# Two-layer masked attention network on one core: where W1's loads and sums are issued in the first steps, and one scaling of Wq folded into a sum

## The chip, the cores and the metric

The kernel runs on one core of one Trainium2 chip. The metric is the device time of one execution in microseconds (us), lower is better. The kernel before was timed three times; the profiled execution is a fourth run with a time of its own.

## What is computed

`x` holds 128 graphs of 128 nodes with 512 features, `adj` one 128x128 mask for each graph. Two layers follow each other:

```python
q = (x @ Wq + bq);  k = (x @ Wk + bk);  v = (x @ Wv + bv)      # 8 heads of 64
logits = einsum('bqhd,bkhd->bhqk', q, k) / sqrt(64)
attn = softmax(where(adj > 0, logits, -1e9), axis=-1)
out = relu(einsum('bhqk,bkhd->bqhd', attn, v) @ Wo + bo)
x = layernorm(x + out)                                         # layer 0

Wh = x @ W1;  s_i = Wh @ a[:512];  s_j = Wh @ a[512:]
e = where(adj > 0, leaky(s_i[:, :, None] + s_j[:, None, :]), -9e15)
x = layernorm(x + leaky(softmax(e, axis=1) @ Wh))              # layer 1
```

Everything is float32.

## The kernel before

**Products.** Every 512x512 weight is cut into four blocks of 256x256, and a product with it is done in seven block products instead of eight, by a Strassen scheme. For this the weight needs three further blocks and one changed one, made once: `right_blocks` (L149 to L156) takes places 0 to 3 (the loaded blocks) and computes `t2 -= t0`, `t5 = t3 - t2`, `t4 = t5 - t0`, `t6 = t1 - t5`, one VectorE instruction each (L152 to L155). `PLACE` says which place each of the seven products reads. The activations need four such sums too (`left_blocks`, L275 to L278), and these are on GpSimd. A chain of seven products writes three PSUM banks, called y, w and x; between products a bank is copied out by ScalarE (`read`, L343 or L347, and L458) or added to such a copy by VectorE (`add`, L384), and TensorE may go on with that bank only after this. For brevity p1, p5, p6, p2, p7, p4, p3 are the products of a chain in their order of issue, and c11, c22, c21, c12 the four results. c22 reads bank w before p3 goes on adding to it.

**Steps.** The main loop (`for t in range(-3, END)`) has one step per graph. Groups of four graphs share the products for Q, K and V (`group_product`, L366, 8 records each of these products in the trace); pairs of graphs share those with Wo and W1 (`pair_product`, L447). A step t issues the scores of graph t (L518), its mask sums, maxima, exponentials (L552), reciprocals (L562) and divisions (L566), stores the softmax weights to DRAM (`sm.store`, L573), fetches them back in another order (`sm.fetch`, L579: `paz`), and in step t + 1 transposes them on VectorE (L583: `paT`) and multiplies them with V (L596). `group()`, `pair()` calls between these pop pieces of the product chains.

**Order.** The order on every engine is the order in which the program issues (`manual_schedule`), so each engine's queue is in order and a waiting instruction holds what stands behind it. All loads and stores but the first four go through SyncE's queue, in program order. One-time work that isn't urgent lies in a list `chores`; `group()` pops two of them at a time in steps t >= 0 (three at t = -3).

**Around the change.**
- W1: `load_w1` (L190) returns ten loads (two broadcasts of the halves of `a`, L196, then eight quarter-column loads of W1, L124) and a list of sums: eight `dots` (L205, two VectorE instructions each with an accumulator read behind each: products of W1's rows with `a`), four `last_column` (L220, two small adds each) and the four block sums. Here W1 is stored with 257 columns per half, the last one holding these dot products, so its block sums are 128x514. The loads go to `chores` at t = 0. The sums are popped by `w1_chores`: four `dots` after the maxima of step 3 and four at its middle, the `last_column` at the middle of step 5, the block sums late in step 5.
- Wv's seven blocks live in DRAM and come back through a ring of three buffers (`wv_n`, L407), fetched ahead of each product.
- Wq: at the start `scale` (L944) multiplies each loaded block by 1/8 on VectorE. `other_half` runs behind the first issued product: it transposes graphs 2 and 3, then scales place 2, makes `t2 -= t0`, issues the four GpSimd sums of x (`add_x`), scales place 3 and makes the other three block sums. In the first group Q's products are issued in the order p1, p2, p5, p6, p7.

Of the kernel before, what the change touches and what calls it, by code (L numbers as in the profile page):

```python
# [24 lines left out]
def kernel(  # L25
# [120 lines left out]

    PLACE = (0, 1, 3, 6, 2, 5, 4)

    def right_blocks(t):  # L149

        return [
            lambda: nc.vector.tensor_sub(t[2], t[2], t[0]),  # L152
            lambda: nc.vector.tensor_sub(t[5], t[3], t[2]),
            lambda: nc.vector.tensor_sub(t[4], t[5], t[0]),
            lambda: nc.vector.tensor_sub(t[6], t[1], t[5]),  # L155
        ]  # L156

    def places(w):
# [31 lines left out]
    def load_w1():  # L190

        a_b = [work.tile([P, D], F32, name="a_b", tag="wh", bufs=4) for _ in range(2)]

        def load_a(s):
            half = a1[s * D : (s + 1) * D].rearrange("f o -> (f o)")
            return lambda: nc.sync.dma_start(a_b[s], half.partition_broadcast(P))  # L196

        loads = [load_a(0), load_a(1)] + block_loads(W1, columns(w1), nc.sync)
        sums = small.tile([P, 2, 2, 2, 2], F32, name="wa", bufs=1)

        def dots(k, o, c):
            def run():
                for s in range(2):
                    scr = work.tile([P, HALF], F32, name="wa_scr", tag="x1S")
                    nc.vector.scalar_tensor_tensor(  # L205
                        scr,
                        w1[:, 2 * o + k, c, :HALF],
                        1.0,
                        a_b[s][:, o * HALF : (o + 1) * HALF],
                        op0=ALU.mult,  # L210
                        op1=ALU.mult,
                        accum_out=sums[:, s, k, o, c : c + 1],
                    )

            return run

        def last_column(k, o):
            def run():
                for c in range(2):
                    nc.vector.tensor_add(  # L220
                        w1[:, 2 * o + k, c, HALF:],
                        sums[:, o, k, 0, c : c + 1],
                        sums[:, o, k, 1, c : c + 1],
                    )

            return run

        every = [(k, o) for k in range(2) for o in range(2)]
        ops = [dots(k, o, c) for k, o in every for c in range(2)]
        return loads, ops + [last_column(k, o) for k, o in every] + right_blocks(places(w1))  # L230

    X, XT, XS, Q, K, V, MF, OT, X1T, X1, WH = ({} for _ in range(11))

# [709 lines left out]
    def scale(n):  # L943
        nc.vector.tensor_scalar_mul(wq[:, n], wq[:, n], QSCALE)  # L944

    wq_sums = right_blocks(places(wq))
    turned = [order_features(b) for b in range(2)]
    keep_busy(14)
# [10 lines left out]
    def other_half():  # L959

        for b in (2, 3):
            transpose_rows(b, order_features(b), nc.scalar.copy)
        scale(2)
        wq_sums[0]()
        add_x()
        scale(3)
        for op in wq_sums[1:]:
            op()

    chores += right_blocks(places(wk)) + load_wv()  # L970
    END = B - GROUP
# [2 lines left out]
    for t in range(-3, END):  # L974
        pair_steps = []
        if t % GROUP == 1 and on(t + 3):
            rest = group_steps
            group_steps, v_pieces, fetch_v = products((t + 3) // GROUP)
            group_steps = rest + group_steps
        if t % 2 == 1 and on(t - 3):  # L980
            pair_steps = zero[(t - 3) // 2] = LayerZero((t - 3) // 2)
            pair_steps = pair_steps.steps()
        if t % 2 == 0 and on(t - 6):
            pair_steps = LayerOne((t - 6) // 2).steps()

        def group(n=1):
            for _ in range(min(n, len(group_steps))):
                group_steps.pop(0)()
            for _ in range(min((3 if t == -3 else 2 if t >= 0 else 1) * n, len(chores))):
                chores.pop(0)()  # L990

        def w1_chores(n):
            for op in [w1_sums.pop(0) for _ in range(n)]:
                op()

        def pair(n=1):
            for _ in range(min(n, len(pair_steps))):
                pair_steps.pop(0)()

        if on(t + 1):  # L1000
            load_mask(t + 1)
        if t == 0:
            load_blocks(Wo, columns(wo), nc.sync, spread_rows=False)
            late_chores = right_blocks(places(wo)) + load_bias()
            w1_loads, w1_sums = load_w1()
            chores += w1_loads
        if t == 1:
            chores += late_chores

        last, sm = sm, Softmax(t, first_homes if t in (0, 2, 4) else None) if on(t) else none  # L1010
        sm.scores()
        coming.turn_blocks()
        if t % 2 == 1 and on(t - 3):
            zero[(t - 3) // 2].by()
            zero[(t - 3) // 2].bw()
        if later and t > 4:
            later.pop().go_back()
        if t == 5:
            group(2)
        if t < 3:  # L1020
            sm.maxima()
            group(2)
            if on(t - 2):
                load_residual(t - 2)
            if t == 0 and on(GROUP):
                sum_x(1)()
            sm.exp(0, 1, 2, 3)
            group()
            sm.reciprocals(0)
            sm.exp(4, 5, 6, 7)  # L1030
            if t == 1:
                group()
            sm.reciprocals(1)
            sm.divide(0, 1, 2, 3)
            last.transpose()
            group()
            sm.divide(4, 5, 6, 7)
            if t == 1:
                group()
            if on(t + 1):  # L1040
                mask_float(t + 1)
        elif t == 4:

            layer = later.pop()
            sm.maxima()
            group()
            layer.apply(0)
            load_residual(2)
            if on(8):
                sum_x(2)()  # L1050
            sm.exp(0, 1)
            group()
            sm.exp(2, 3, 4, 5)
            last.transpose()
            group()
            layer.store(1)
            layer.store(0)
            layer.fetch(1)
            layer.fetch(0)
            sm.exp(6, 7)  # L1060
            group()
            sm.reciprocals(0)
            sm.reciprocals(1)
            sm.divide(0, 1, 2, 3, 4, 5, 6, 7)
            mask_float(5)
        else:
            sm.maxima()
            group()
            if t == 3:
                w1_chores(4)  # L1070
            if t == 5:
                turn_x1(4)
                x1_sums()
            edge = coming
            edge.add()
            fin.residual()
            if on(t - 2):
                load_residual(t - 2)
            edge.maxima()
            fin.stats()  # L1080
            fin.rstd()
            x1_sums()
            if t % GROUP == 0 and on(t + GROUP):
                sum_x(t // GROUP + 1)()
            pair()
            sm.exp(0, 1, 2, 3)
            edge.exp()
            if t in (3, 5):
                w1_chores(4)
            pair()  # L1090
            sm.exp(4, 5)
            last.transpose()
            group()
            sm.reciprocals(0)
            pair()
            sm.exp(6)
            fin.apply()
            fin.store()
            sm.exp(7)
            edge.divide()  # L1100
            pair()
            sm.reciprocals(1)
            sm.divide(0, 1, 2, 3)
            coming = Edge(t - 6) if on(t - 6) and t + 1 < END else none
            coming.sender()
            coming.store_sender()
            if t == 5:
                w1_chores(4)
            group()
            sm.divide(4, 5)  # L1110
            pair()
            sm.divide(6, 7)
            if on(t + 1):
                mask_float(t + 1)
            group()
        sm.store()
        if t >= 6:
            coming.fetch_sender()
        sm.fetch()
        for b in x_turns(t):  # L1120
            transpose_x(b)
        for b in x_turns(t + 1):
            load_x(b)
        if on(t + 1):
            mask(t + 1)
        pair(2)
        if t % 2 == 0 and on(t - 6):
            turn_x1(t)
        if t not in (0, 4):
            group(21 if t % GROUP == 0 else 1)  # L1130
        fin = edge
        fin.product()
        fin.copy()

        last.attend()
        last.copy()
        if t % 2 == 0:
            last.sum(0, 1, 2, 3)
# [183 lines left out]
```

## Time and profile before

| | |
|---|---|
| three timed runs | 2402.37 us median (2400.96 to 2404.64) |
| profiled execution | 2402.25 us, of which 2400.4 us are the profile's span |
| TensorE matmul / weight load busy | 98% / 82% of the span |
| VectorE, ScalarE, GpSimd busy | 76%, 63%, 34% |
| data moved | 395.32 MB, 165 GB/s on average |

The page gives busy times of the engines, a chain of what ended last, groups of instructions and DMA issues. The waits view names, for an engine, what it waited for, with the total, the count and the longest. The timeline lists instructions in order: start in us, duration in us, engine, line, operation, tile written <- tiles read, shape, count, and in brackets the idle time before it with its releaser. The windows view gives busy time of each engine in a stretch, then the granted TensorE clock as a share of full speed, the DMA engines' busy share and GB/s. In the trace tile names have lost their digits, so W1 is `w`, and the layer-0 buffers X1 are `x`. Scores of step 0 begin at 41.0 us, of step 1 at 49.2, step 2 at 69.3, step 3 at 80.6, step 4 at 102.3, step 5 at 111.6 and step 6 at 132.9.

### The profile page before, as it was taken

Reading aid. Unit: us, or ns where it says so; the run is one execution under the profiler, and the core shown is the slowest. Engines: PE = TensorE matmul, PEld = TensorE weight load, DVE = VectorE, ACT = ScalarE, POOL = GpSimd, SP = SyncE. Lnnn points to the kernel's source line nnn. Section 1 sums busy time; section 2 is a strip of 40 time slices with the busy share of each in tenths; the row PEclk is TensorE's granted clock in tenths of the full one; section 3 lists DMA queues with packets and bytes.
Section 4 is the critical chain, followed back from the end, with each engine's and each line's share of the span. In section 5 each row is a group of like instructions: output and inputs, shape, how many; then the busy total and the mean of one; then the engine's idle time right before and its main releaser. Section 6 shows DMA issues by size and latency. Waiting matters only on the chain.

```text
span 2400.4 us, 44153 instructions
## 1 busy us (share of the span) xinstructions
PE 2363.4 (98%) x13362; PEld 1980.3 (82%) x13362; DVE 1827.0 (76%) x3719; ACT 1517.3 (63%) x5463; POOL 811.1 (34%) x1195
## 2 busy tenths in 40 slices
PE   8999999999999999999999999999999999999996
PEld 7888888888888888888888888888888888888874
DVE  5677787777777877877777778778778777777777
ACT  3666666566666666665666666666666666666685
POOL 1232333233333333332333433333323334333335
PEclk9999999999999999999999999999999999999999
DMA  7455555555546545555545555555554554554452
GB/s 205 158 165 160 174 163 162 176 161 158 179 147 186 164 154 174 160 165 181 159 154 183 154 176 167 156 173 157 169 181 157 157 179 155 173 175 151 156 170 98
DMA packets 435566, 395.32 MB, mean 165 GB/s; under 512 B 108280, under 2 KB 339328, under 8 KB 435328
## 3 DMA queue, kind: packets, MB, share of 16 engines
q1 hardware_dynamic: 435008, 392.23, 52.3%
q8 instruction: 107, 1.75, 0.3%
q14 instruction: 131, 1.07, 0.1%
q10 hardware_dynamic: 320, 0.26, 0.0%
HBM read 248.58 MB, written 143.72 MB: 163 GB/s over the span
## 4 chain that ended last, share of the span: by engine, by line
PE 91%; DVE 3%; DMA 2%; ACT 2%; issue 1%; SPq 1%; POOL 1%; DVEq 0%; ACTq 0%; POOLq 0%
PE st_y L366 27%; PE p_y L447 17%; PE st_w L366 13%; PE p_w L447 9%; PE st_x L366 7%; PE lg L518 6%; PE p_oT L596 5%; PE p_x L447 4%; PE p_h L837 4%; DMA wv_n<-wv 1%; ACT pa L552 0%; DMA x_dram<-x 0%; DMA wq<-in_L_gnn_Wq_dram 0%; ACT pa L566 0%; POOL rstd L648 0%
## 5 line engine op out<-in xcount | busy, mean ns | idle before, releaser
L552 ACT ACTIVATE pa<-pa,nmax 128x128 f32<-128x128 f32 x1008 | 392.6, 393 | 5.9 <-DVE nmax L541 5.5
L646 POOL TENSOR_SCALAR ve<-mv 128x1 f32<-128x1 f32 x256 | 69.9, 273 | 855.9 <-DVE mv L642 847.1
L566 ACT ACTIVATE pa<-pa,rs 128x128 f32<-128x128 f32 x1008 | 334.1, 395 | 8.6 <-DVE rs L562 8.5
L275 POOL TENSOR_TENSOR oS<-oT 128x256 f32<-128x256 f32 x63 | 45.8, 727 | 643.4 <-ACT oT L610 643.4
L532 DVE TENSOR_TENSOR pa<-lg,mf 128x512 f32<-128x512 f32 x252 | 161.9, 684 | 99.9 <-PE lg L518 99.6
L458 ACT COPY pr_t<-p_y 128x257 f32<-128x257 f32 (+1 forms) x375 | 137.7, 367 | 135.7 <-PE p_y L447 133.3
L343 ACT COPY st_t<-st_y 128x512 f32<-128x512 f32 x192 | 110.5, 575 | 144.2 <-PE st_y L366 143.1
L552 ACT ACTIVATION_READ_ACCUMULATOR pa<-pa,nmax 128x1 f32 x1008 | 192.3, 191 | 0.0
L347 ACT ACTIVATE st_t<-st_y,b_cols 128x256 f32<-128x256 f32 x192 | 80.6, 471 | 164.9 <-PE st_y L366 164.9
L648 POOL TENSOR_TENSOR rstd<-ve,mhalf 128x1 f32<-128x1 f32 x256 | 177.0, 691 | 21.4
L596 PEld LDWEIGHTS p_oT<-paT,v 128*64 128x64 f32 x2016 | 107.5, 136 | 91.8 <-PE st_y L366 44.0
L610 ACT ACTIVATE oT<-p_oT,b_cols 128x128 f32<-128x128 f32 x504 | 144.2, 368 | 60.0 <-PE p_oT L596 58.9
L583 DVE STREAM_TRANSPOSE paT<-paz 128x1024 f32<-128x1024 f32 x126 | 156.9, 1245 | 3.3 <-DMA paz<-pa_dram 2.1
L541 DVE TENSOR_REDUCE nmax<-pa 128x8 f32<-128x1024 f32 x126 | 153.7, 1220 | 4.4
L518 PE MATMUL lg<-kT,qT 64*128 64x128 f32 x2048 | 148.7, 285 | 0.0
L518 PEld LDWEIGHTS lg<-kT,qT 64*128 64x128 f32 x2048 | 124.2, 187 | 22.9 <-issue 22.9
L596 PE MATMUL p_oT<-paT,v 128*64 128x128 f32 x2016 | 137.9, 279 | 0.3 <-DVE paT L583 0.3
L768 DVE TENSOR_TENSOR wh<-p_w,pr_t 128x257 f32<-128x257 f32 x122 | 51.9, 425 | 104.0 <-PE p_w L447 64.1
L447 PE MATMUL p_y<-wo,oT 128*128 128x256 f32 x504 | 129.9, 380 | 0.7 <-ACT pr_t L458 0.6
L447 PE MATMUL p_y<-wo,oS 128*128 128x256 f32 x504 | 129.4, 379 | 0.0
L447 PE MATMUL p_y<-w,x1T 128*128 128x257 f32 x496 | 128.2, 381 | 0.2 <-DVE x1T L245 0.2
L447 PE MATMUL p_y<-w,x1S 128*128 128x257 f32 x496 | 128.0, 380 | 0.0
(201 smaller groups left out, 6032.8 us busy)
## 6 DMA issues: line engine op xcount, KB each, us to landing
pa_dram<-pa SPq DMA_DIRECT2D x126, 512.0 KB, 3.0
paz<-pa_dram SPq DMA_DIRECT2D x504, 128.0 KB, 2.8
wv_n<-wv SPq DMA_DIRECT2D x224, 256.0 KB, 2.8
x<-in_x_dram SPq DMA_DIRECT2D x128, 256.0 KB, 2.9
x_dram<-x SPq DMA_DIRECT2D x128, 256.0 KB, 2.5
xz<-x_dram SPq DMA_DIRECT2D x512, 64.0 KB, 2.0
xz<-in_x_dram SPq DMA_DIRECT2D x496, 64.0 KB, 2.2
out_dram<-z SPq DMA_DIRECT2D x120, 256.0 KB, 2.3
```

The lines of the kernel that those rows point to most:

```text
L366: nc.tensor.matmul(p[:, m, :], lhs, rhs, start=start and m == 0 and kc == 0, stop=True, skip_group_check=True,)
L447: nc.tensor.matmul(p[:, :width], xs()[n][:, kc, :], w[:, PLACE[n], kc, :], start=start and kc == 0, stop=True, skip_group_check=True,)
L458: nc.scalar.copy(t[:, :width], p[:, :width])
L518: nc.tensor.matmul(self.lg[r][:, c, :], q[rows, c, cols], k[rows, c, cols], start=c == 0, stop=True, skip_group_check=True,)
L532: nc.vector.tensor_add(by_head[:, r * NC : (r + 1) * NC], self.lg[r].rearrange("p c (b k) -> p c b k", b=4), mf.unsqueeze(1).to_broadcast( ...
L541: nc.vector.tensor_reduce(self.nmax, by_head, AX.XY, ALU.max, negate=True)
L552: nc.scalar.activation(self.pa[:, :, h, :], self.pa[:, :, h, :], AF.Exp, bias=self.nmax[:, h : h + 1], accum_out=self.sums[:, h : h + 1],)
L566: nc.scalar.activation(self.pa[:, :, h, :], self.pa[:, :, h, :], AF.Copy, scale=self.rs[:, h : h + 1])
L583: nc.vector.transpose(self.paT.rearrange("p h (a i) -> p a h i", i=32), self.paz.rearrange("p a (h k) -> p a h k", k=32),)
L596: nc.tensor.matmul(self.oT[r * HD : (r + 1) * HD, c, :], v[:, h * HD : (h + 1) * HD], self.paT[:, r * NC + c, :], start=c == 0, stop=True, ...
L610: nc.scalar.activation(OT[pair][:, c, h * P : (h + 1) * P], self.oT[:, c, :], AF.Identity, bias=b_cols[:, 1, c : c + 1],)
L648: nc.gpsimd.tensor_tensor(self.r, ve, mhalf, ALU.pow)
```

## The change

Four edits, all in what is issued before step 6:
1. W1's loads leave `chores`. Four are issued behind the store of the softmax weights of step 0, four behind that of step 1, the last two behind that of step 2; in each step ahead of the fetch.
2. W1's `dots` are done in three places: three after the maxima of step 3, two late in step 3 (behind the divisions of heads 0 to 3), three at the end of the first half of step 4. Since each pops two instructions, these are 6, 4 and 6 VectorE instructions. The four `last_column` move to late in step 5.
3. W1's four block sums are issued on GpSimd, right behind the `last_column`.
4. For Wq, the scalings of places 2 and 3 are folded into the sums that follow them: t2 and t5 each become one instruction that multiplies by 1/8 and subtracts. Place 3 is still scaled, now after all sums. The GpSimd sums of x are issued behind the first of the two.

```diff
-    def right_blocks(t):
+    def right_blocks(t, engine=nc.vector):
 
         return [
-            lambda: nc.vector.tensor_sub(t[2], t[2], t[0]),
-            lambda: nc.vector.tensor_sub(t[5], t[3], t[2]),
-            lambda: nc.vector.tensor_sub(t[4], t[5], t[0]),
-            lambda: nc.vector.tensor_sub(t[6], t[1], t[5]),
+            lambda: engine.tensor_sub(t[2], t[2], t[0]),
+            lambda: engine.tensor_sub(t[5], t[3], t[2]),
+            lambda: engine.tensor_sub(t[4], t[5], t[0]),
+            lambda: engine.tensor_sub(t[6], t[1], t[5]),
         ]
...
-        return loads, ops + [last_column(k, o) for k, o in every] + right_blocks(places(w1))
+        ops += [last_column(k, o) for k, o in every]
+        return loads, ops, right_blocks(places(w1), nc.gpsimd)
...
+    def scaled_less(n, left, right):
+
+        nc.vector.scalar_tensor_tensor(
+            wq[:, n], wq[:, left], QSCALE, wq[:, right], op0=ALU.mult, op1=ALU.subtract
+        )
+
...
             transpose_rows(b, order_features(b), nc.scalar.copy)
-        scale(2)
-        wq_sums[0]()
+        scaled_less(2, 2, 0)
         add_x()
+        scaled_less(5, 3, 2)
+        for op in wq_sums[2:]:
+            op()
         scale(3)
-        for op in wq_sums[1:]:
-            op()
...
-            w1_loads, w1_sums = load_w1()
-            chores += w1_loads
+            w1_loads, w1_sums, w1_blocks = load_w1()
...
             layer.fetch(0)
+            w1_chores(3)
             sm.exp(6, 7)
...
             if t == 3:
-                w1_chores(4)
+                w1_chores(3)
...
             edge.exp()
-            if t in (3, 5):
-                w1_chores(4)
             pair()
...
             coming.store_sender()
+            if t in (3, 5):
+                w1_chores(2 if t == 3 else 4)
             if t == 5:
-                w1_chores(4)
+                for op in w1_blocks:
+                    op()
             group()
...
         sm.store()
+        if 0 <= t < 3:
+            for load in w1_loads[4 * t : 4 * t + 4]:
+                load()
         if t >= 6:
             coming.fetch_sender()
         sm.fetch()
```

## The prediction

> **What bounds the kernel now.** I read first the windows of the whole run, since the change touches only the first 135 us and I must know whether a gain there survives.
>
> ```profile
> 60.00:180.00 120.00, 115.61 (x670) 97.81 (x670) 84.02 (x185) 75.46 (x282) 31.94 (x42) 0.98 0.51 162
> 180.00:2280.00 2100.00, 2099.46 (x11937) 1767.30 (x11936) 1620.24 (x3287) 1343.15 (x4868) 713.18 (x1029) 1.00 0.53 166
> 2280.00:2400.40 120.40, 97.94 (x517) 73.10 (x515) 92.40 (x202) 80.26 (x262) 54.59 (x110) 0.95 0.40 133
> ```
>
> The second column is the length, the third TensorE's busy time. From 180 to 2280 us TensorE is idle for 0.54 us in all: a TensorE-bound stretch, in which an earlier start is kept. Only its idle time and its slow clock before that can be won. Second, TensorE's waits in the first 200 us:
>
> ```profile
> PE st_w L366 <- DVE kT L384: 2.8, 1, 2.8
> PE st_w L366 <- DMA wv_n<-wv: 2.8, 1, 2.8
> PE st_w L366 <- DMA wk<-in_L_gnn_Wk_dram: 2.6, 1, 2.6
> ```
>
> Three waits of 2.6 to 2.8 us; all others are below 1.4. Third, the timeline around each, VectorE and GpSimd at the start, then SyncE and TensorE at 46, then VectorE and TensorE at 92:
>
> ```profile
> 12.03 1.33 DVE L944 TENSOR_SCALAR wq<-wq 128x512 f32<-128x512 f32 x1 [2.26 <-DMA wq<-in_L_gnn_Wq_dram]
> 13.39 1.63 DVE L152 TENSOR_TENSOR wq<-wq 128x512 f32<-128x512 f32 x1
> ...
> 18.13 0.69 DVE L154 TENSOR_TENSOR wq<-wq 128x512 f32<-128x512 f32 x1
> ```
>
> ```profile
> 46.24 0.91 SPq L196 DMA_DIRECT2D a_b<-in_L_gnn_a_dram  x2
> 47.20 0.90 SPq L124 DMA_DIRECT2D w<-in_L_gnn_W_dram  x2
> 48.20 0.37 SPq L407 DMA_DIRECT2D wv_n<-wv  x1
> ```
>
> ```profile
> 56.05 2.67 PE L366 MATMUL st_w<-wv_n,xT 128*128 128x256 f32 x8 [2.78 <-DMA wv_n<-wv]
> 58.51 2.92 PE L366 MATMUL st_y<-xT,wq 128*128 128x256 f32 x8
> ```
>
> ```profile
> 92.04 0.42 DVE L205 SCALAR_TENSOR_TENSOR wa_scr<-w,a_b 128x256 f32<-128x256 f32 x1
> 92.39 0.08 DVE L205 DVE_READ_ACCUMULATOR wa_scr<-w,a_b 128x1 f32 x1
> 92.39 1.24 DVE L583 STREAM_TRANSPOSE paT<-paz 128x1024 f32<-128x1024 f32 x1
> 93.55 0.65 DVE L384 TENSOR_TENSOR kT<-st_w,st_t 128x512 f32<-128x512 f32 x1
> ```
>
> The first wait is put down to a DMA, but st_w at 15.12 reads place 2 of Wq, ready at 13.39 + 1.63 = 15.02: it is VectorE's chain. The second is the last Wv block, issued behind four W1 loads and landing after 7.7 us where the median of its kind is 2.8. The third is K's c22, behind sixteen dot products on VectorE. After each of the three the windows show a granted clock of 0.5 for about 3 us, and none after the waits of 0.9 and 1.0 us at 51 and 21 us.
>
> **What the Trainium skill says.**
> - "TensorE: Matmul & The Clock Gate", Part 1: the array's clock halves after an idle window of about 3.4 us, which runs freely, and comes back after about as much work. The trace agrees on half and on the recovery (0.50 between 57 and 60 us), but waits of 2.6 to 2.8 us are already enough here.
> - "DMA: Bandwidth & Descriptors", Queues, rings and completion order: descriptors on one DMA engine are taken in ring order, so on SyncE's queue an earlier load goes first. The 7.7 us agree.
> - "SBUF — State Buffer", Who interferes with whom: a VectorE instruction with two SBUF inputs and a GpSimd instruction that reads SBUF exclude each other; the second one waits. The trace agrees: the 128x512 subtraction took 1.63 us beside GpSimd's sums of x, 0.69 after them.
> - "GPSIMD Engine Reference", section 3: a tensor_tensor is about 2 times slower there. In the trace GpSimd's 128x512 sums take 1.27 us alone, against 0.69.
>
> **The change, part by part.** Times are those of the profiled execution (2402.25 us).
>
> *Wq.* Until 17.5 us GpSimd is busy with four sums (ends 13.07, 14.47, 16.15, 17.55), and VectorE's four instructions end 0.3 to 0.55 us behind these ends: it advances one instruction for each GpSimd sum, whatever its kind. So I take the folded instructions at the same pace, and not at their bare 0.69: t2 ends at 13.6 instead of 15.02, t5 at 15.0 instead of 18.09, t4 at 16.7, t6 at 18.1, the scaling 0.38 later. p5 starts at 13.7 (TensorE free since 12.49, a wait of 1.2 us, too short to halve the clock), p6 at 15.45, p7 after ScalarE's copy (0.98 us as before) at 18.2 instead of 21.86. Two products follow, 1.73 each in the chain, then p3 would start at 23.4. It needs c22, which stands behind ten VectorE instructions that do not change: the first of these starts at 18.5 instead of 19.34, so c22 ends at 25.93 - 0.84 = 25.1. So p3 starts at 25.2 instead of 27.11. **Gain 1.9 us**; a new wait of 1.8 us takes part of it. Bounds: 1.2 if that wait slows the clock, 3.2 if the folded instructions run near 0.7 us.
>
> *W1's loads.* Gone from before the Wv fetch: it then waits for its ring buffer, free when the product at 45.67 ends (47.4), and lands 2.8 us later at 50.2. p3 of V needs it, and c22, which ended at 51.94, and TensorE, which is free at 53.0 (51.27 + 1.73). So 53.0 instead of 56.05: 3.05 us. The two products behind it take 2.67 and 2.71 in the chain instead of 1.73 each: 1.92 more. **Gain 5.0 us.**
> Where the ten loads go: behind the stores of steps 0, 1, 2, ahead of the fetches on the same queue. SyncE waits there anyway (5.1 us at step 0 for the store to land), so their issue, 0.47 us each, is covered. Their bytes aren't: 768, 512 and 256 KB are moved before `paz`. At step 0, in the shifted time: store at 53.17 - 1.9 = 51.3, landing with 3.0 us at 54.3, fetch issued to 56.0; the store's bytes are through near 53.4, W1's follow at some 220 GB/s (the windows of 51 to 55 us), so 768 KB end near 57; 512 KB of `paz` at 288 GB/s (the window of 56 us, mostly a store) end near 58.7, and with an estimated 1 us of the 2.8 that a 256 KB block needs alone they land near 59.7; `paT` ends at 60.9. TensorE reaches the product with it at 68.3 - 6.9 = 61.4. **Cover 0.5 us**: without it, each us later costs a us, and a wait of 2.6 or more another 1.9. At step 1 `paT` is held by the reciprocals (71.2, shifted), and `paz` lands near 69; at step 2 it lands near 79.7 and VectorE isn't ready before 80.1. The ten loads cost nothing else, since W1 is first read at step 3; the third `dots` needs the last two loads, issued at 74, landing by 77 and read at 79.
>
> *W1's sums.* Of sixteen instructions (0.467 us from start to start) ten leave the first place: 4.67 us less ahead of `paT` and c22. c22 is then done at 89.5 in the old time; TensorE is free at 91.43 and started at 94.26. **Gain 2.83 us**, and the clock: st_w and the next product took 3.38 and 1.17 instead of 1.73 and 0.86: 1.96. **Together 4.8 us.** The four in the second place (1.87 us) fall into VectorE's wait of 2.33 us for ScalarE at 94.7. The six of step 4 (2.8 us) come behind the V sum at 109.6; c22 of V (111.27) and the reciprocals get 1.2 us later, and behind them ScalarE's divisions and bias copies (115.96 to 117.2; the product that needs the first copy starts at 117.94, so 0.35 us remain). The store of step 4 waits until 116.67 for SyncE itself, not for ScalarE. Cost 0, up to 1 us.
> The last columns take 1.14 us at 125.6, where 2.73 us of block sums go away. On GpSimd the blocks take 4 x 1.35 = 5.4 us, 126.8 to 132.2. The first product with a changed block is at 136.7. Behind them GpSimd has the rstd of step 5 (132.39), on which VectorE waits: 0 to 1 us there.
>
> **Sum.** 1.9 + 5.0 + 4.8 = 11.7; I take off 0.7 for the thin covers (0.5 at step 0, 0.2 on GpSimd): 11.0. From the profiled 2402.25 (0.12 below the median) this gives 2391.3 us. Own range: gain 8.5 to 14.5, 2387.8 to 2393.8.
>
> **Rivals.**
> 1. *The fetch of step 0 inherits the wait.* If the loads ahead of `paz` land as slowly as W1's did before (7.2 us), `paT` is some 3 us late, TensorE waits that long and its clock halves: 3 + 1.9 = 4.9 back, **2396.2**. For: 0.5 us of cover. Against: some 2.2 MB were issued between 45.8 and 53.5 us then, onto a queue that was still busy; now 1.3 MB lie ahead of the fetch, on one that is empty.
> 2. *The shift is lost to waits of the later first steps* (ScalarE's copies at step 4, rstd at step 5, c22 at the start with a halved clock): 7 to 9 us of the 11.7 come back, **2399.5**, no change by measurement. For: three covers below 1 us. Against: the other engines get earlier with TensorE.
> 3. *Slower: the stalls were what gave the other queues their lead.* If, without them, SyncE's ring of Wv blocks trails TensorE in every later group, the wait seen once at 179.3 us (0.66 us for `wv_n`) returns in each of some 29 groups: 19 us lost against 11 won, **2410**. It decides from 0.55 us per group on (15.8 us, gain and bound together). Against: from 180 to 2280 us VectorE, the busiest of the others, is idle for 23%, so they catch up.
> 4. *It doesn't do what it says*: the first wait is really the DMA of Wk. Then 1.9 goes, 2393.2, inside the forecast.
>
> **How the numbers follow.** A measurement of this kernel tells about 0.2% (4.8 us) from no change. Forecast 0.73 (with rival 4), rival 1 0.14, rival 2 0.08, rival 3 0.05. Forecast and rival 1 are faster: 0.87; same 0.08; slower 0.05. The range reaches from 2387.8 over rival 1 to 2396.8; it leaves out rivals 2 and 3.
>
> **What would show it.** Right: in the first 200 us no TensorE wait above 2 us, no halved clock after 13 us, the last Wv block of group 0 landing in under 3.5 us, step 6's scores near 122 us instead of 132.9, 180 to 2280 us unchanged. Wrong: a wait of the L596 product for `paT` at 60 us, a wait at c22 of more than 2.6 us at 24, waits for `wv_n` that recur. The largest risk is the landing of `paz` at step 0.

## The result, and the profile after

The changed kernel takes 2394.41 us in the median of 7 runs (2392.07 to 2398.11), the kernel before 2402.89 us beside it (2400.96 to 2405.53): ratio 0.9961 with an interval of 0.9952 to 0.9971, 8.5 us less. The profiled execution took 2394.42 us (span 2392.5) where before's took 2402.25 (span 2400.4): 7.83 us less. The forecast was 2391.3: less time, as said, and by more than the timed runs scatter, with 3.1 us missing. The time lies inside the whole range and just outside the forecast's own one (up to 2393.8).

The windows of the changed kernel, in the same columns as before (stretch, length, then busy us and instructions of PE, PEld, DVE, ACT, POOL, then granted clock, DMA share, GB/s):

```profile
60.00:180.00 120.00, 118.55 (x711) 99.80 (x711) 83.37 (x183) 75.05 (x277) 37.83 (x47) 1.00 0.59 179
180.00:2280.00 2100.00, 2098.72 (x11910) 1766.07 (x11909) 1624.50 (x3297) 1345.97 (x4880) 716.05 (x1034) 1.00 0.53 165
2280.00:2392.50 112.50, 89.92 (x477) 66.76 (x475) 84.85 (x184) 73.69 (x236) 50.68 (x104) 0.95 0.42 135
```

In the first line TensorE is busy for 2.9 us more of the 120, at full clock. In the second it idles for 1.28 us where it idled for 0.54: a small loss in the part that the change doesn't touch. TensorE's waits in the first 200 us (in total, times, longest):

```profile
PE st_w L367 <- DVE qT L385: 1.8, 1, 1.8
...
PE st_w L367 <- DVE wq L949: 1.2, 1, 1.2
...
PE p_oT L597 <- DVE paT L584: 0.5, 2, 0.3
```

The three waits of 2.6 to 2.8 us are gone. In their place stand 1.2 us for Wq's folded place 2, 1.8 us for c22 (both were forecast with these sizes), and 0.5 us in two waits for `paT`. In the first 200 us no stretch behind 13 us shows a halved clock. The timeline of the two products behind the former wait for `wv_n`, then of K's former wait for c22 (start, length, operation; a bracket would give the wait before it):

```profile
51.85 1.89 PE L367 MATMUL st_w<-wv_n,xT 128*128 128x256 f32 x8
53.57 1.89 PE L367 MATMUL st_y<-xT,wq 128*128 128x256 f32 x8
...
84.79 1.03 PE L448 MATMUL p_y<-wo,oS 128*128 128x256 f32 x4
85.65 1.89 PE L367 MATMUL st_w<-xT,wk 128*128 128x256 f32 x8
```

No bracket is left on either, and the products are at full-clock lengths (1.89 where 2.67 and 2.92 stood). The last Wv block landed in 3.0 us instead of 7.7.

To see where the time comes from I use the start of the scores product (`lg<-kT,qT`) of each step: its gain is the start in the first trace of before minus the start in the other trace. In the profiled pair:

| | step 0 | 2 | 4 | 6 | 7 | 127 | whole run |
|---|---|---|---|---|---|---|---|
| before, at us | 41.02 | 69.28 | 102.35 | 132.9 | | | |
| after, at us | 39.77 | 63.66 | 91.95 | 122.35 | | | |
| gain | 1.25 | 5.62 | 10.40 | 10.55 | 9.78 | 8.52 | 7.83 |

So the change had won 10.55 us by step 6, and gave 2.7 us of it back: 0.77 between steps 6 and 7, 1.26 in the 120 steps behind, 0.6 to 0.7 in the tail.

### The profile page after: what moved, and what is told of

Its sections match the earlier page's. It is cut to its first block, busy times and chain, and to the rows that moved or that the text cites. A ratio compares the mean times of both kernels' runs of the same rounds, so it can differ in the third digit from the quotient of the medians.

```text
span 2392.5 us, 44154 instructions
## 1 busy us (share of the span) xinstructions
PE 2360.1 (99%) x13362; PEld 1977.5 (83%) x13362; DVE 1824.9 (76%) x3714; ACT 1517.4 (63%) x5463; POOL 816.4 (34%) x1199
## 4 chain that ended last, share of the span: by engine, by line
PE 88%; ACT 3%; DMA 3%; DVE 3%; SPq 1%; issue 1%; POOL 1%; DVEq 0%; ACTq 0%; POOLq 0%
PE st_y L367 26%; PE p_y L448 17%; PE st_w L367 13%; PE p_w L448 8%; PE st_x L367 6%; PE lg L519 5%; PE p_oT L597 5%; PE p_h L838 4%; PE p_x L448 4%; ACT pa L553 1%; ACT pa L567 1%; DMA x_dram<-x 1%; SPq L241 0%; DMA wv_n<-wv 0%; DVE pa L533 0%
```

## The experiments

Two things were open. Which of the three edits won what, and are the waits that they remove worth what I took them for, clock included? And where does the time that is missing go: to the fetch of step 0 (rival 1), to the later first steps and GpSimd (rival 2), or to a lead that the other queues lost (rival 3)? All gains below are those of the score starts against the first trace of before. A ratio compares timed runs with those of the kernel before made beside them; a trace is one execution, and not always a typical one: that of e10 is the slowest of its 15 runs (2402.5 us, median 2398.1), that of e8 the slowest of 6 (2399.7, median 2394.5).

One term in advance. Where the granted clock is halved, it stays so for 3.41 us, or for two or three times that, in every stretch read here. A TensorE that is busy throughout loses half of 3.41, so 1.7 us. I call this a half window; where TensorE waits in it anyway, less is lost.

| kernel | ratio to before (95%) | step 0 | 2 | 4 | 6 | 7 | 127 |
|---|---|---|---|---|---|---|---|
| changed, first trace | 0.9961 [0.9952, 0.9971] | 1.25 | 5.62 | 10.40 | 10.55 | 9.78 | 8.52 |
| e1 Wq only | 0.9998 [0.9989, 1.0006] | 1.12 | 3.75 | 3.76 | 4.05 | 4.05 | -0.96 |
| e2 loads only | 0.9991 [0.9982, 0.9999] | 0.32 | 3.47 | 2.13 | 2.49 | 2.50 | 0.40 |
| e3 sums and blocks only | 0.9981 [0.9974, 0.9988] | -3.27 | -1.30 | 3.49 | 4.21 | 3.44 | 0.30 |
| e4 blocks on VectorE | 0.9965 [0.9952, 0.9978] | 1.33 | 5.34 | 10.13 | 10.18 | 10.06 | 6.69 |
| e5 before, again | 1.0001 [0.9990, 1.0012] | 0.45 | 2.45 | 2.45 | 2.01 | 1.96 | -0.48 |
| e6 changed, again | 0.9968 [0.9960, 0.9976] | 0.76 | 4.48 | 9.27 | 9.30 | 8.52 | 6.07 |
| e7 all loads at step 0 | 0.9986 [0.9980, 0.9993] | 0.89 | 0.48 | 3.42 | 3.22 | 2.45 | 0.40 |
| e8 c22 first | 0.9954 [0.9938, 0.9969] | 1.82 | 5.52 | 10.31 | 10.60 | 9.81 | 4.01 |
| e9 c22 first, blocks on VectorE | 0.9962 [0.9949, 0.9974] | 2.12 | 5.88 | 10.67 | 9.95 | 9.84 | 9.76 |
| e10 e9, loads behind the fetch | 0.9979 [0.9971, 0.9986] | 2.27 | 6.97 | 6.71 | 5.88 | 5.76 | 1.10 |
| e11 changed, third time | 0.9971 [0.9961, 0.9981] | 0.61 | 4.90 | 9.69 | 9.88 | 9.12 | 8.61 |

**Wq's folding alone (e1).**

```diff
...
-        scale(2)
-        wq_sums[0]()
+        scaled_less(2, 2, 0)
         add_x()
+        scaled_less(5, 3, 2)
+        for op in wq_sums[2:]:
+            op()
         scale(3)
-        for op in wq_sums[1:]:
-            op()
```

> Only the two folded scalings of Wq are taken over from the change. Theory (three separate gains that add up): the scores of step 0 and of step 6 start 1.25 us earlier than before (39.8 and 131.6 us), the waits of 2.8 us at 56 and at 94 us stay, the time is 1.2 us lower, too little to be told from noise. Rival (the first gain is swallowed by the waits that follow): step 6 starts at 132.9 as before.

Measured: ratio 0.9998 [0.9989, 1.0006]; step 0 1.12 us earlier. The first wait changes as in the full change, here in the waits of the first 150 us of e1:

```profile
PE st_w L366 <- DVE kT L384: 2.8, 1, 2.8
PE st_w L366 <- DMA wv_n<-wv: 1.8, 1, 1.8
PE st_w L366 <- DVE qT L384: 1.8, 1, 1.8
PE st_w L366 <- DVE wq L948: 1.2, 1, 1.2
```

The wait of 2.6 us, which the profile booked to the DMA of Wk, became one of 1.2 us for `wq` although no DMA was changed: it was VectorE's chain, and rival 4 falls. The wait for c22 of 1.8 us comes with it. And the wait for `wv_n` fell to 1.8 us, with no halved clock behind it: an earlier TensorE does not fully add to the next wait, so the gains of single edits are not independent.

**W1's loads alone (e2).**

```diff
-            chores += w1_loads
...
         sm.store()
+        if 0 <= t < 3:
+            for load in w1_loads[4 * t : 4 * t + 4]:
+                load()
```

> Only W1's ten loads are moved behind the stores of steps 0 to 2; its sums stay on VectorE where they were. Theory: the wait for the last Wv block goes, step 2 starts 4.4 us earlier (64.9 us), the wait for K's c22 at step 3 stays with 2.8 us and a halved clock, step 6 at 128.5, time 2398. Rival (with the earlier start the fetch of step 0 or the last W1 loads become late): step 4 has won less than 3 us.

Measured: 0.9991 [0.9982, 0.9999]. The wait for `wv_n` is gone and step 2 starts 3.47 us earlier, of which 3.15 come between steps 1 and 2. At step 0 TensorE waits 1.48 us for `paT`, though W1's loads lie ahead of the fetch in the changed kernel too, where it waits 0.3 to 0.9; why this fetch lands later here isn't shown. Then 1.35 us are lost between steps 3 and 4, which the edit doesn't touch. The rival's sign, less than 3 us won at step 4, came true (2.13), so in part by the late fetch that the rival names and in part by the clock. The window of e2 there:

```profile
90.00:97.00 7.00, 6.23 (x15) 4.98 (x16) 4.09 (x12) 3.38 (x11) 0.00 (x0) 0.51 0.19 77
```

The wait for c22 (2.8 us) is as long as in before, but here the clock was halved for 6.8 us, two half windows instead of one.

**W1's sums and blocks alone (e3)**: the changed kernel with the old Wq chain and the old place of the loads (against the changed kernel; the Wq lines, which go back to those of before, are left out).

```diff
             w1_loads, w1_sums, w1_blocks = load_w1()
+            chores += w1_loads
...
-        if 0 <= t < 3:
-            for load in w1_loads[4 * t : 4 * t + 4]:
-                load()
```

> Only W1's sums are spread over three places and its block sums moved to GpSimd; the loads stay ahead of the Wv fetch, Wq as before. Theory: the waits at 15 and 56 us stay, c22 at step 3 is in time, step 4 starts 4.8 us earlier (97.6 us), step 6 at 128.0, time 2397.5. Rival (the sixteen instructions were covered by the loads' delay): step 4 has won less than 3 us.

Measured: 0.9981 [0.9974, 0.9988]. Between steps 3 and 4 it gains 4.79 us, and the changed kernel's three traces gain 4.78 each: the predicted 4.8. Step 0 is 3.27 us *later* than in before, with the same code up to there. Its window and TensorE's timeline at the start:

```profile
16.00:28.00 12.00, 10.34 (x28) 7.46 (x27) 9.49 (x14) 1.68 (x4) 1.78 (x2) 0.57 0.66 187
```

```profile
18.56 3.75 PE L367 MATMUL st_y<-xS,wq 128*128 128x256 f32 x8 [0.69 <-DVE wq L153]
```

Eight matmuls took 3.75 us instead of 1.97: a granted clock of 0.57 over the 12 us, where before's has 0.86. The waits in there are of 0.7 and 1.0 us. The clock was halved for three windows in a row (10.2 us) where before had one. The two more are worth up to 3.4 us, and e3's start is 0.3 us later (GpSimd's first sum at 12.12 us instead of 11.81); step 0's 3.27 lies within that. With the same code up to there, this is the clock's doing and not the edit's.

**Both kernels again (e5 before, e6 and e11 changed), without an edit**, to see how far two traces of one kernel lie apart.

> The kernel before once more, for its trace. If the 2 us that the changed kernel lost between steps 6 and 127 are small waits for data that vary from execution to execution, the starts of the scores in this trace drift against those of the first trace by about a us between step 6 and step 127, with no trend. If they agree within 0.2 us, the loss belongs to the change.

> The changed kernel once more, for its trace. Step 6 starts again at 122.4 us within 0.3. If the loss behind it is chance, the losses at steps 17, 21 and 105 (0.5 to 0.7 us each) aren't at the same steps again; if the change makes them, they are.

> The changed kernel a third time, beside the two others on the same chip. Step 6 at 122.4 to 123.7 us, a loss of 1 to 3 us against the first trace of before behind step 7, at steps 17, 21, 29 or 105 as in the other traces, no halved clock before step 7.

Measured: 1.0001 [0.9990, 1.0012] for the kernel before, 0.9968 [0.9960, 0.9976] and 0.9971 [0.9961, 0.9981] for the changed one. In the trace of e5 step 2 starts 2.45 us earlier than in the first trace of the same kernel. TensorE behind the wait for `wv_n` in e5:

```profile
55.28 1.96 PE L366 MATMUL st_w<-wv_n,xT 128*128 128x256 f32 x8 [2.46 <-DMA wv_n<-wv]
57.08 1.89 PE L366 MATMUL st_y<-xT,wq 128*128 128x256 f32 x8
```

The wait is there (2.46 against 2.78 us), the halved clock isn't; the same products took 2.67 and 2.92 us in the first trace. The window of the same four microseconds, first before and then e5:

```profile
57.00:61.00 4.00, 4.00 (x12) 3.23 (x11) 2.18 (x4) 0.15 (x2) 0.00 (x0) 0.57 0.30 98
```

```profile
57.00:61.00 4.00, 4.00 (x21) 3.51 (x20) 3.65 (x7) 1.99 (x9) 0.00 (x0) 1.00 0.41 132
```

TensorE is busy for 4.00 us in both, with 12 instructions in one and 21 in the other: PE's busy share cannot show such a loss, the clock column does. So in the first 140 us before loses three half windows in one execution and one in another; the changed kernel lost none there in three.

Two expectations were missed. e5 drifts by 2.5 us between steps 6 and 127, and not by about one. Step 6 of e6 starts at 123.60 us, 1.2 later than in the first trace of the changed kernel: 0.5 of it are there at step 0, 0.6 come with the wait for `paT`. And e6 loses time at steps 21 and 105 again, which by the text put down before it speaks for the change; but e5, the kernel before, loses at steps 17, 21 and 41 too.

**W1's four blocks on VectorE (e4)**, the rest as changed.

```diff
-        return loads, ops, right_blocks(places(w1), nc.gpsimd)
+        return loads, ops, right_blocks(places(w1))
```

> The changed kernel with W1's four block sums back on VectorE, late in step 5. If GpSimd's sums are what made VectorE 0.9 us late at step 6 and cost 0.7 us of TensorE time between steps 6 and 7, the mask sum of step 6 starts 3.0 us behind its scores (as before the change) and not 3.9, and step 7 comes 17.0 us after step 6, not 17.8. If the late load of x at step 5 is the cause, it stays at 3.9 and 17.8. Time 2394 in both cases.

Measured: 0.9965 [0.9952, 0.9978], and from step 6 to step 7 17.15 us. This distance parts the kernels: 17.02 to 17.15 in all seven with the blocks on VectorE (before, e5, e1, e2, e4, e9, e10), 17.79 to 17.82 in the six with them on GpSimd. GpSimd's blocks thus cost about 0.7 us. The path of it: GpSimd in the changed kernel, then VectorE in the changed kernel, then VectorE in e4:

```profile
116.92 1.09 POOL L153 TENSOR_TENSOR w<-w 128x514 f32<-128x514 f32 x1 [0.16 <-DVE w L220]
118.09 1.10 POOL L154 TENSOR_TENSOR w<-w 128x514 f32<-128x514 f32 x1
119.15 1.46 POOL L155 TENSOR_TENSOR w<-w 128x514 f32<-128x514 f32 x1
122.72 0.22 POOL L647 TENSOR_SCALAR ve<-mv 128x1 f32<-128x1 f32 x1 [2.11 <-DVE mv L643]
```

```profile
117.65 0.42 DVE L694 TENSOR_TENSOR pr_t<-p_w,pr_t 128x256 f32<-128x256 f32 x1 [0.87 <-ACT pr_t L459]
118.79 0.68 DVE L683 SCALAR_TENSOR_TENSOR x<-pr_t,x 128x256 f32<-128x256 f32 x1 [0.71 <-DMA x<-in_x_dram]
```

```profile
118.83 0.42 DVE L683 SCALAR_TENSOR_TENSOR x<-pr_t,x 128x256 f32<-128x256 f32 x1
```

GpSimd idles for 2.11 us before `ve`, the first instruction towards rstd: the blocks did not delay it. What is late is VectorE's `x<-pr_t,x`. It could start at 118.07, ends at 119.47, 0.28 us behind the end of GpSimd's third sum (118.09 + 1.10 = 119.19), and takes 0.68 us; the profile books the idle 0.71 us to the load of `x`. In e3, another trace with GpSimd's blocks, it starts without a wait, takes 1.36 us, and ends again 0.28 us behind the end of such a sum (124.44 + 1.09); in e11 and e6, the other two traces of the changed kernel, it ends 0.28 us behind the third sum as well (after 1.36 us without a wait, and after 0.80 us behind a wait of 0.60). Beside no GpSimd sum it takes 0.42 us (e4 and before). From there the lateness runs over the transposes, the mask sum of step 6 (3.9 us behind its scores, 3.3 in e4, where 3.0 was expected), the maxima and ScalarE's exponentials to the copy into `pr_t`, and TensorE's p_y waits for that: two such products start 0.2 and 0.7 us later behind the scores than in e4. In e4 VectorE does four sums more and is still earlier. By time e4 can't be told from the changed kernel.

**All ten loads behind the store of step 0 (e7).** This doubles and more what lies ahead of the fetch of step 0.

```diff
-        if 0 <= t < 3:
-            for load in w1_loads[4 * t : 4 * t + 4]:
+        if t == 0:
+            for load in w1_loads:
```

> The changed kernel with all ten W1 loads behind the store of step 0, so 1.5 MB instead of 0.77 ahead of the fetch on the queue. Theory (that fetch has almost no cover left): 768 KB more at 220 GB/s and six more issues make the attention product of step 0 wait about 3.5 us instead of 0.27, the clock halves behind it, and step 3 starts 4 to 5.5 us later than in the changed kernel (75.0 us); time 2399. Rival (the fetch doesn't stand behind the loads' bytes): the wait stays under 1.5 us.

Measured: 0.9986 [0.9980, 0.9993], and step 3 at 81.94 instead of 74.96 us, 7.0 us later. The product with `paT`, first in the changed kernel and then in e7, and e7's window around it:

```profile
62.64 1.09 PE L597 MATMUL p_oT<-paT,v 128*64 128x128 f32 x16 [0.27 <-DVE paT L584]
```

```profile
66.89 1.98 PE L597 MATMUL p_oT<-paT,v 128*64 128x128 f32 x16 [4.16 <-DVE paT L584]
```

```profile
65.00:73.00 8.00, 6.11 (x38) 5.17 (x39) 5.86 (x9) 2.07 (x7) 0.00 (x0) 0.57 0.57 187
```

The wait grew from 0.27 to 4.16 us, and behind it two half windows of clock were lost (3.4 us): 3.9 + 3.4 = 7.3, against 7.0 seen. The wait is near the 3.5 us expected, but one half window was expected and two came. So the cover of the fetch of step 0 is used up in the changed kernel: the six loads more ahead of it were paid in full. That is rival 1's mechanism, at a load that the change itself doesn't reach.

**c22 ahead of other sums (e8).** Two sums of Wk's blocks, on which K's first product doesn't yet wait, go behind Wv's steps.

```diff
-        chores += right_blocks(places(wk)) + load_wv()
+        wk_sums, wv_steps = right_blocks(places(wk)), load_wv()
+        chores += wk_sums[:2] + wv_steps + wk_sums[2:]
```

> The changed kernel with two of Wk's block sums moved behind Wv's, so that c22 of the first group stands behind eight VectorE instructions instead of ten. Theory: c22 ends 1.4 us earlier, TensorE's wait of 1.8 us at 25.8 shrinks to 0.4 to 0.6, step 0 starts at 38.4, step 6 at 121.1, time 2393. Rival (VectorE then waits for Wv's loads, or the first Wv block comes too late): step 0 has won less than 0.5 us.

Measured: 0.9954 [0.9938, 0.9969]; the wait for c22 falls from 1.82 to 0.83 us (0.4 to 0.6 expected), and step 0 starts 1.82 us earlier than in before, although GpSimd's first sum of x began only at 12.39 us (11.81 in before, 11.96 in the first trace of the changed kernel; why this start counts is said below). The new wait of 1.8 us was thus the next limit, and about 1 us of it can be had. By time e8 can't be told from the changed kernel beside it (0.9968 [0.9960, 0.9976]).

**Both (e9), and with the loads behind the fetch (e10).** e10 is e9 with the loop of loads one line lower:

```diff
         sm.store()
-        if 0 <= t < 3:
-            for load in w1_loads[4 * t : 4 * t + 4]:
-                load()
         if t >= 6:
             coming.fetch_sender()
         sm.fetch()
+        if 0 <= t < 3:
+            for load in w1_loads[4 * t : 4 * t + 4]:
+                load()
```

> The changed kernel with c22 of the first group behind two VectorE instructions fewer and with W1's block sums on VectorE. From the traces of these two edits alone: step 0 starts about 1.05 us earlier than in the changed kernel on the same DMA timing, and the 0.77 us between steps 6 and 7 are not lost, so step 7 starts 1.5 to 1.8 us earlier (about 138.5 us); time 1.5 us lower, below what the timed runs can tell apart. If the two gains are taken back by the attention product of step 0, whose fetch can't start earlier, its wait grows by as much.

> As the kernel before it, and W1's loads are issued behind the fetch of each step instead of ahead of it. Theory (the fetch of step 0 waits for the bytes of 768 KB in front of it): paz lands in under 4 us instead of 5, the wait of 0.3 to 0.9 us at the attention products of steps 0 and 1 falls to 0.3 together, the last loads still come before the sums of step 3. Rival (the loads now delay the loads of x and the Wv fetch behind them): new waits at steps 2 to 4 of 0.5 us or more. Time 2394, or 0.5 to 1 us below the kernel before it.

Measured: e9 2392.41 us, 0.9962 [0.9949, 0.9974]; it has the shortest span of all traces (2390.6), but its interval overlaps those of the changed kernel, beside it 0.9971 [0.9961, 0.9981]. It is ahead at step 4 (10.67) and, with the blocks off GpSimd, loses only 0.11 us from step 6 to 7; between 5 and 6 it loses 0.72, where p_y waited 1.08 us for ScalarE's copy. That wait is 0.3 to 1.1 us in eleven other traces and absent in e3. Step 7 comes at 140.1 us where 138.5 was expected.

e10 takes 2398.06 us, 5.7 more than e9; in its trace, a slow one, it is 4.0 us behind e9 at step 4. Its rival came true. At step 0 it is what rival 1 asks for: the fetch lands in 2.4 to 2.8 us, TensorE doesn't wait for it, and step 2 starts at 62.31, the earliest of all (gain 6.97). But at step 2 the store and the fetch of SyncE's queue:

```profile
75.21 0.32 SPq L574 DMA_DIRECT2D pa_dram<-pa  x1
...
79.99 1.74 SPq L580 DMA_DIRECT2D paz<-pa_dram  x4
```

The fetch is issued 4.8 us behind the store (3.1 in e9), late in the step, and step 4 has a gain of only 6.71. K waits 2.0 us for c22 once more. So of the two places tried, the one in which SyncE waits for its store to land is the better; that the loads behind the fetch are what makes the next store land late is read from this order, not tested apart.

## Why the prediction was right, and where it was off

- **The bound.** Right. Time won in the first steps was kept where TensorE is the bound: 10.55 us at step 6, 8.52 us at step 127.
- **Wq: 1.9 forecast, 1.25, 0.76 and 0.61 measured** in the three traces of the changed kernel, 1.12 in e1. The order of events was as worked out: VectorE advances by one instruction for each of GpSimd's four sums, TensorE waits 1.2 us at Wq and 1.8 for c22, no clock is halved. Mis-sized is the pace. The prediction let the sums end where they ended before, whatever VectorE does beside them. GpSimd's second sum, in before and in the changed kernel:

```profile
13.15 1.32 POOL L276 TENSOR_TENSOR xS<-xS,xT 128x512 f32<-128x512 f32 x1
```

```profile
13.31 1.60 POOL L277 TENSOR_TENSOR xS<-xS,xT 128x512 f32<-128x512 f32 x1
```

  It stood behind a scaling, which has one input; now it stands behind a folded instruction, which has two and takes longer (0.69 against 0.42 us alone). The fourth sum grows in the same way, from 1.32 to 1.59. So the exclusion of the two engines, which the prediction quotes for VectorE, holds GpSimd up as well, and the four sums take 6.28 us instead of 5.74: 1.6 for these two in all nine traces with the folding, 1.3 in all four without. The rest is the start. GpSimd's first sum begins at 11.81 us in the first trace of before, the earliest of thirteen, at 11.96, 12.46 and 12.60 in those of the changed kernel and at 12.10 in e1. With this taken off, all four gains are 1.40 or 1.41: 0.5 us short by the pace, the remainder by a start that I took for fixed. The timed ratio of e1 can't tell this edit from nothing.
- **Loads: 5.0 less 0.5 forecast; between steps 1 and 2 4.36, 3.78 and 4.53 measured.** The wait for `wv_n` went, its block landed in 3.0 us (2.8 forecast), and 3.05 us of wait and one half window of clock were won against the first trace. Against e5, which has no halved window there, it is 2.0 us less: that this term came out so well is in part the luck of the trace that it was both priced from and compared with. The issue of the fetch ended at 56.65 us instead of 56.0, and `paz` was there 4.5 us later where 3.7 was estimated, at 61.2 instead of 59.7. In e10, with no loads ahead, `paT` can start 2.5 us behind that issue. This used up the cover: TensorE waits of 0.27, 0.91 and 0.34 us for `paT` in the three traces. The 0.5 us taken off were about right.
- **Sums: 4.8 forecast, 4.78 measured**, in every trace that has all of it, but for e10 (1.5), and in e3, where it is alone. It contains 1.96 us for the clock, and the clock did halve in all four traces with this wait (before, e1, e2, e5). The six instructions at step 4 cost nothing that shows: step 6 keeps step 4's gain (10.40 and 10.55).
- **GpSimd's blocks: 0.2 taken, 0.77 measured; the step that failed.** The prediction had the cost, up to 1 us, on rstd, and looked only at GpSimd's own queue. The runs show GpSimd idle before rstd and VectorE's `x<-pr_t,x` held by the sums. The Trainium skill, "SBUF — State Buffer", Who interferes with whom, says just that of a VectorE instruction with two SBUF inputs beside a GpSimd instruction that reads SBUF; I quoted it for the start of the kernel and didn't apply it to the four instructions that the change moves to GpSimd. The miss at Wq is of the same kind: each time one engine's ends were taken as given while the other's work beside it changed.
- **180 us and on, "unchanged": not quite.** From step 7 to 127 the first trace of the changed kernel gives back 1.26 us. That this is the change isn't shown: the other two give back 2.45 and 0.51, and the kernel before lost 2.44 in e5 against its own first trace. Every other trace loses something there too, 0.08 (e9) to 5.80 us (e8), mostly at the same steps (17, 21, 29, 41 and 105), and the longest waits are for `wv_n`. These waits from 150 to 2280 us, in e5 (before again) and in e8:

```profile
PE st_y L366 <- DMA wv_n<-wv: 1.9, 3, 1.0
```

```profile
PE st_y L367 <- DMA wv_n<-wv: 3.3, 4, 1.1
```

  Rival 3's wait exists, then, but 2 to 6 times in a trace and not in each of 29 groups, and with the kernel before as well. That it isn't the earlier start which brings it is read from these traces; another ring buffer for `wv_n`, which would test it, wasn't tried.
- **Which case came true.** By mechanism the forecast, by size between it and rival 1 (2396.2). Of the 11.0 us forecast, the profiled pair lacks 0.65 at Wq, 0.14 at the loads, 0.6 at the blocks, 1.26 behind step 7 and 0.6 to 0.7 in the tail, some 0.15 were won between steps 4 and 6: together 3.1. The mean gain of the three traces of the changed kernel over the two of before is 8.9 us at step 6 and 8.0 at step 127; the timed ratios give 7 to 9.4.
- **The tail: 0.6 us not forecast.** It is the clock again. About 65 us before the end TensorE waits 2.39 us for ScalarE's copy of p_y, in before and in the changed kernel alike:

```profile
2335.19 1.13 PE L447 MATMUL p_y<-wo,spare 128*128 128x256 f32 x4 [2.39 <-ACT p_y L468]
```

```profile
2326.67 2.08 PE L448 MATMUL p_y<-wo,spare 128*128 128x256 f32 x4 [2.39 <-ACT p_y L469]
```

  All thirteen traces have this wait, and in eight a half window follows it: in the three of the changed kernel, but not in the two of before, nor in e9, whose code is the changed kernel's there. From the scores of step 127 to the end it is 85.7 us in before, e5 and e9, and 86.3 to 86.8 in the three. So the loss goes with the halved window; that the change brings it isn't shown.
- **What stays open.** Which part of the losses behind step 7 is chance, why the fetch of step 0 lands later in e2, and how single edits add: they sum to 7.3 us by their ratios (0.5, 2.2 and 4.6) against 7.0 to 9.4 together, and with intervals of 2 us each no more can be said.

## What to carry to other kernels

A TensorE wait of 2.5 us or more in a TensorE-bound kernel is worth its length and, more often than not, half a clock window besides, so price it from several traces and not from the one in which it halved. When sums move to GpSimd, or VectorE's instructions beside them change, list which of the two engines then waits for which, not only what queues behind them on GpSimd. Two-input instructions are not the only ones: the one-input scalings of before took 1.33 and 1.48 us beside GpSimd's sums, and 0.42 without. Put extra DMA issues where the queue's engine waits anyway, and then work out whose landing their bytes delay: past the cover each microsecond is paid, with the clock on top.

## What was not expected of the hardware

- The clock changes on a grid, and a window of it needs to be idle only in part. In each of the thirteen traces all changes of the granted clock lie a whole multiple of 3.413 us behind the first one, to within 0.005 us. Add up TensorE's idle time in each of these windows, some 9100 from the first full clock on. Where the clock was full, every window idle for 59% or more (2.0 us; there are 32) was followed by a halved one, and none idle for 58% or less. So it matters where a wait falls. Of eleven waits of 2.5 to 2.8 us in the first 140 us of all traces, eight were followed by halved windows and three weren't, since they lay across a border of the grid; of the waits of up to 2.0 us none was. The wait for `wv_n` in before, and in e5, each with the grid window that holds most of it (length, then TensorE's busy time):

```profile
53.74:57.16 3.42, 1.11 (x5) 1.04 (x6) 1.69 (x2) 1.80 (x9) 0.00 (x0) 1.00 0.98 251
```

```profile
51.32:54.73 3.41, 1.49 (x7) 0.96 (x6) 2.60 (x5) 1.40 (x5) 0.00 (x0) 1.00 1.11 201
```

  TensorE is idle for 67% of the first and 56% of the second; the first was followed by a halved window, the second wasn't. The Trainium skill, "TensorE: Matmul & The Clock Gate", Part 1, has the clock halve after an idle window of about 3.4 us, which runs freely. The length and the grid agree; an idle window in full wasn't needed here.
- It need not come back after one window. Behind a halved window with 12% of idle time or less it did, behind one with 18% or more it didn't: it stayed halved for two windows behind the wait of 4.16 us in e7 and behind one of 2.8 us in e2, and for three at the start of e3, with TensorE working in between and waits of 0.7 and 1.0 us.
- VectorE's wait for GpSimd shows in the profile in two guises: as a longer instruction (1.36 us instead of 0.42 in e3) or as idle time put down to another releaser (0.71 us to the load of `x` in the changed kernel). What gives it away is the end, 0.28 us behind that of GpSimd's instruction in both, and in e6 and e11 too.
